# A two-layer convolution kernel: expert products placed ahead in the first image, Newton square roots, a second chunk buffer, and small moves in four queues

## The chip, the cores and the metric

One Trainium2 chip, one of its cores. The number that counts is the device time of one execution in microseconds, the median of several runs of the same program. A profile is one further execution, recorded instruction by instruction; its own time is given beside its span.

## The reference, cut to what matters

The input `x` has the shape (4, 64, 256, 256): four images of 64 channels. Everything is float32.

```python
# layer 0, on the group norm of x (32 groups, per image)
h = gelu(conv3x3(x)); xa, k = split(conv1x1(h))
xs = gelu(conv3x1(conv1x3(xa)))                    # one filter for each channel
mask = top2(softmax(mean(xs) @ gate_w.T))          # per image, three experts
out = xs + sum_i mask[i] * c1x1(c1x1(k) * c1x1(xs)) # inner widths 2, 4, 8
x = x + conv1x1(out)
# layer 1, on the group norm of the new x (per image)
h = relu(batchnorm(conv3x3(x, quantized w1)))      # statistics over all four images
h = batchnorm(conv3x3(h, quantized w2))
x = x + relu(h + identity)
```

The quantized weights are scaled by the largest absolute weight over 127, rounded, clipped and scaled back. A group norm divides by the square root of a variance; there are eight of these in all (four images in each layer), and two batch norms.

## The kernel before, in words

**Stages.** The program runs through them once: statistics of image 0 (to about 52 us of the span); the *front* of layer 0 for 64 units of 16 rows, 16 units for each image (57 to about 1310 us, the last units overlapping the next stage); the first convolution of layer 1, in 64 chunks of 8 row pairs, called conv1 (1271 to 1960 us); batch norm; the second convolution (1970 to 2520 us); and an end stage that only streams (to 2958 us). PE is the matrix engine, DVE the vector engine, ACT the scalar engine, POOL the fourth compute engine. DMA transfers are issued by SP and, for a few stores, by ACT.

**An order written by hand.** `at(step, order, call)` puts a call into a table, and the table is executed sorted by `(step, order)`; every engine, SP's queue among them, keeps that order. `at_slot(u, pos, call)` is the same in slots: slot `u` is two steps, and `pos` runs from 0 to 12 within it. So a position in the table fixes where an instruction stands among the others of its own engine; when it runs is decided by the waits. A chain such as `stats_end` is a generator: each `next` in the table runs it to its next `yield`.

**One slot of the front.** PE does, in this order: products (1, 2) and (3, 4) of the transformed convolution (pos 1 and 1.3, `front_conv`, 24 + 24 matmuls, tile `ps_c`, two buffers); the first rounds of the taps of unit u-2 (pos 2, `front_taps_a`, tile `ps_a`, one buffer); their last rounds (pos 4, `front_taps_b`); products (0, 5) into the bank of (3, 4) (pos 5); the first rounds of unit u-1 (pos 7); in even slots `front_k` and in odd slots `front_q` (pos 8, tiles `ps_k` and `ps_q`, in the one buffer of tag "p"); the last rounds of unit u-1 (pos 9). Each `front_taps_b` waits for a memset, called the tick (`divide`, L506), which waits for the last matmul of the `front_taps_a` before it. The tick is on DVE in image 0 and on POOL afterwards.

The other engines' part of a slot: DVE combines the products (`butterfly_a` to `_d`, L631 to L650; `butterfly_c`, pos 4.05, has to be done before products (0, 5) are added to its bank), finishes the taps (`front_taps_h`, L706, L714, L717; the last of them frees `ps_a`), and takes half of the next image's statistics in image 0 (`stats_group`, `bn_stats`, L415). ACT copies and scales (L547, L570, L572, L626), starts the taps (L699), applies gelu (L658, L730), and takes the rest of the statistics (`stats_piece`, L448). POOL makes the input transform (L553 to L596).

From slot 20 on (`u >= NCH + 4`) the output of the image before runs in the same slots: tiles `y` (two buffers) are loaded from `in_xp`, added to, and stored to `y_d`. There `ps_o` also needs tag "p".

**Layer 1's weights** are quantized on DVE in `weights1`, a chain of three parts, for `w1` in slots 7 to 9 and for `w2` in slots 10 to 12, at pos 7.3. The middle part holds three operations on 128x768 (L253, L254, L255).

**Square roots.** `combine` averages over a group by two small matmuls and ends with Sqrt on ACT (L282) and a reciprocal on DVE (L284). It is called by `stats_end` (layer 0's norm), `group_norm` in `out_end` (layer 1's norm) and `bn_affine`.

**conv1.** For each chunk: `conv1_load` (tile `yn`, by SP), differences on POOL (L343), upper and lower halves on ACT and DVE (L930, L359, L346; L362, L353), 36 matmuls (`ps_hm`, `ps_h`, L296), the result on DVE (`leave`, L318), squares on ACT (L382) and a store of the result to `h1_d` by ACT's queue (L998). The result tile is `h1` of `conv1_pool`, one buffer, or, for odd chunks from the fourth on, the place of `chunk_x`. The output of image 2's last third and of image 3 runs beside conv1 (`plan_out_late`): `out_slot` about every fourth step, and `out_store` (L893) by SP one step after each second `out_slot`. The last slots of the front (`TAIL`) run beside the first chunks.

## Time and profile before

| | us |
|---|---|
| median of 3 runs | 2964.82 |
| lowest, highest | 2963.71, 2973.92 |
| the profiled execution | 2959.65 |
| its span, first to last instruction | 2957.8 |
| PE, DVE, ACT, POOL busy | 2345.4, 2448.4, 2007.1, 1676.8 |

The profiled execution lies 5.2 us below the median of the runs. A busy share is an average over stages with different limits; what a change in one stage is worth is read in that stage. In the timeline rows a line gives start, duration, engine, line of the source and the tiles written and read; brackets give the idle time of the engine before it and what ended that. In the table by stretch each engine's busy time stands beside the length of the stretch.

### The profile page before, as it was taken

To read this page: it belongs to the slowest core of one execution; us is meant where nothing else is said; L and a number is where in the kernel's file an instruction comes from. 1 tells how busy PE (TensorE), PEld (TensorE's weight loads), DVE (VectorE), ACT (ScalarE), POOL (GpSimd) and SP (SyncE) were. 2 spreads that over 40 slices of the span, in tenths; PEclk is the share of its full clock that TensorE was granted. 3 is DMA by queue.
4 is the path that set the end of the run, shared out by engine and by line. 5 is a ranking of instruction groups with operands and counts; after the bars stand their busy time and mean duration, and the time that the engine had idled before them with its cause. 6 is when DMAs were issued, how large, how long until landed. Compare 5 with 4: busy or idle time off the path is not lost.

```text
span 2957.8 us, 52737 instructions
## 1 busy us (share of the span) xinstructions
PE 2345.4 (79%) x21576; PEld 1502.1 (51%) x21576; DVE 2448.4 (83%) x2811; ACT 2007.1 (68%) x2183; POOL 1676.8 (57%) x1252
## 2 busy tenths in 40 slices
PE   2888899999999999979999999989999999000000
PEld 1444445444445555546666667867788888000000
DVE  6688678888888988869999999979999898976664
ACT  4777888787776665567676667978888887432221
POOL 6988888787778888733545546735555555000000
PEclk9999999999999999999999999999999999555555
DMA  8665579999999999859999997747777764999999
GB/s 352 233 239 209 199 269 369 354 351 350 355 349 320 320 319 327 290 203 320 343 367 361 332 360 272 270 176 274 258 267 264 270 219 156 375 412 423 420 424 409
DMA packets 135715, 915.35 MB, mean 309 GB/s; under 512 B 14960, under 2 KB 15728, under 8 KB 40880
## 3 DMA queue, kind: packets, MB, share of 16 engines
q1 hardware_dynamic: 107824, 777.74, 71.1%
q10 hardware_dynamic: 27648, 134.23, 11.3%
q8 instruction: 170, 2.79, 0.4%
q14 instruction: 73, 0.60, 0.1%
HBM read 573.74 MB, written 338.17 MB: 308 GB/s over the span
## 4 chain that ended last, share of the span: by engine, by line
PE 50%; DMA 29%; DVE 13%; ACT 3%; POOL 2%; issue 2%; SPq 0%; ACTq 0%; DVEq 0%; POOLq 0%
PE ps_h L296 18%; PE ps_c L513 9%; DMA y<-in_xp 7%; PE ps_a L513 7%; PE ps_h2m L296 6%; DMA y_end<-y_d 5%; DMA y_d<-y 4%; DMA out<-h 4%; DMA h<-h_d 4%; PE ps_o L513 4%; DMA yn<-y_d 3%; PE ps_hm L296 3%; DVE t L714 2%; DVE t L717 2%; PE ps_k L744 1%
## 5 line engine op out<-in xcount | busy, mean ns | idle before, releaser
L296 PE MATMUL ps_h<-diff,w_q 128*128 128x512 f32 x3072 | 755.2, 400 | 12.4 <-DVE h L318 11.9
L296 PEld LDWEIGHTS ps_h<-diff,w_q 128*128 128x128 f32 x3072 | 577.0, 189 | 190.6 <-issue 20.4
L513 PE MATMUL ps_c<-v,us 64*64 64x256 f32 x9216 | 534.0, 380 | 28.6 <-DVE ps_c L644 25.4
L343 POOL TENSOR_TENSOR d<-yn 128x1024 f32<-128x1024 f32 x128 | 348.9, 2745 | 299.3 <-DMA yn<-y_d 164.8
L513 PEld LDWEIGHTS ps_c<-v,us 64*64 64x64 f32 x9216 | 360.7, 134 | 174.4 <-issue 17.6
L343 POOL TENSOR_TENSOR d<-h 128x1024 f32<-128x1024 f32 x126 | 307.1, 2459 | 206.4 <-DVE diff L351 143.6
L513 PE MATMUL ps_a<-h,av 64*64 64x512 f32 x4080 | 386.5, 492 | 47.3 <-DVE t L717 40.1
L318 DVE SCALAR_TENSOR_TENSOR h<-ps_h,scale_w,m 128x1024 f32<-128x1024 f32 x256 | 323.1, 1279 | 78.7 <-PE ps_h L296 56.3
L561 POOL TENSOR_TENSOR x<-x 128x512 f32<-128x512 f32 x256 | 328.8, 1284 | 12.7
L1497 ACT ACTIVATE h<-h,shift,gn 128x2048 f32<-128x2048 f32 (+1 forms) x65 | 134.3, 2067 | 276.0 <-DVE h L1496 273.8
L513 PEld LDWEIGHTS ps_a<-h,av 64*64 64x64 f32 x4080 | 153.7, 133 | 322.2 <-issue 212.8
L382 ACT ACTIVATE junk<-h,less_h 128x2048 bf16<-128x2048 f32 (+3 forms) x134 | 256.2, 1912 | 13.6 <-DVE h L318 13.5
L1496 DVE SCALAR_TENSOR_TENSOR h<-h,inverse,y_end 128x2048 f32<-128x2048 f32 (+1 forms) x65 | 150.5, 2317 | 122.0 <-DMA y_end<-y_d 122.0
L699 ACT ACTIVATE t<-ps_a,tap_bias,m 128x1016 f32<-128x1016 f32 x128 | 153.3, 1197 | 117.0 <-PE ps_a L513 91.4
L880 DVE SCALAR_TENSOR_TENSOR y<-ps_o,ob,y 128x1024 f32<-128x1024 f32 x128 | 164.0, 1281 | 50.9 <-PE ps_o L513 26.6
L730 ACT ACTIVATE xs<-t 128x1024 f32<-128x1024 f32 x128 | 134.8, 1053 | 103.8 <-DVE t L717 90.2
L353 DVE SCALAR_TENSOR_TENSOR diff<-d,gn,diff 128x1024 fp32r<-128x1024 f32 x128 | 202.0, 1608 | 0.9 <-ACT diff L346 0.5
L296 PE MATMUL ps_h2m<-odd,w_q 128*128 128x512 f32 x768 | 193.5, 401 | 5.9 <-ACT odd L359 3.8
L296 PE MATMUL ps_hm<-odd,w_q 128*128 128x512 f32 x768 | 194.0, 402 | 2.8 <-DVE t L717 1.3
L346 ACT ACTIVATE diff<-d 128x1024 fp32r<-128x1024 f32 x128 | 135.3, 1057 | 81.1 <-POOL d L343 79.5
L553 POOL TENSOR_TENSOR x<-x,x 128x512 f32<-128x512 f32 x128 | 160.5, 1275 | 34.2 <-ACT x L547 34.2
L717 DVE SCALAR_TENSOR_TENSOR t<-ps_a,m,t 128x1020 f32<-128x1020 f32 x128 | 163.9, 1280 | 4.6
(256 smaller groups left out, 4235.2 us busy)
## 6 DMA issues: line engine op xcount, KB each, us to landing
x<-in_xc SPq DMA_DIRECT2D x64, 1280.0 KB
h<-h_d SPq DMA_DIRECT2D x64, 1152.0 KB
yn<-y_d SPq DMA_DIRECT2D x60, 1152.0 KB
xs_in<-in_xp SPq DMA_DIRECT2D x64, 1024.0 KB
xs_d<-xs ACTq DMA_DIRECT2D x128, 512.0 KB
xs_in<-xs_d SPq DMA_DIRECT2D x64, 1024.0 KB
y<-in_xp SPq DMA_DIRECT2D x64, 1024.0 KB
y_d<-y SPq DMA_DIRECT2D x64, 1024.0 KB
```

The lines of the kernel that those rows point to most:

```text
L296: nc.tensor.matmul(ps, wq[w][:, kind, kx, :], t[:, rows, kx : kx + W], start=(j == 0), stop=(j == len(terms) - 1))
L318: nc.vector.scalar_tensor_tensor(h.rearrange("p (e k) w -> p e (k w)", e=2), ps.rearrange("p e k w -> p e (k w)"), w_scale[w], m.unsqueeze ...
L343: engine.tensor_tensor(raw.rearrange("p (g r) w -> p g r w", g=2), *pair, ALU.subtract)
L353: nc.vector.scalar_tensor_tensor(lower, raw, scale, upper.bitcast(F32), ALU.mult, ALU.subtract)
L382: nc.scalar.activation(junk[rows, 0:n], flat(h), AF.Square, bias=less[name][rows], accum_out=total)
L513: last[:] = [nc.tensor.matmul(ps[o, at_out[0] : at_out[1], :], w[i], rhs[i], **flags)]
L553: nc.gpsimd.tensor_tensor(x4[:, j - 1], x_rows(u, j + 2), x4[:, j - 1], ALU.subtract)
L561: nc.gpsimd.tensor_tensor(x[:, r : r + 2], x[:, r + 2 : r + 4], x[:, r : r + 2], ALU.subtract)
L699: nc.scalar.activation(t[:, :, inside], ps[:, :, inside], AF.Identity, bias=tap_bias, scale=sh[:, 1:2])
L717: nc.vector.scalar_tensor_tensor(t[:, :, 0 : W - 1], ps[:, :, 1:W], sh[:, 2:3], t[:, :, 0 : W - 1], ALU.mult, ALU.add)
L880: nc.vector.scalar_tensor_tensor(y, ps.rearrange("p x s w -> p x (s w)"), out_bias[b], y, ALU.add, ALU.add)
L1496: nc.vector.scalar_tensor_tensor(at_h, at_h, inverse[:, b : b + 1], y[:, a:e, :], ALU.mult, ALU.add)
```

## The change

It has seven parts.

1. In slots below 20, `front_k` stands at 4.5, between `front_taps_b` and products (0, 5), instead of 8; three quarters of `front_q` (units 0 to 2) stand at 4.5 too, and the last quarter stays at 8.
2. In image 0 the first `bn_stats` pair of a slot stands at 6.125 (behind `butterfly_d`) instead of 4.1.
3. `weights1` yields after each of its three large operations; it runs in slots 5 to 8 (`w1`) and 9, 10, 11, 14 (`w2`).
4. For images 1 to 3 of layer 0's norm and all four of layer 1's, the square root and reciprocal become a first guess on DVE (two operations, one of them on the bits as an integer) and three Newton steps of three operations each on POOL. Image 0's norm and the batch norms keep Sqrt. The chains get one more place each, and some places move.
5. Chunk 1 of image 0 in conv1 writes its result to the place of `chunk_x` too.
6. For that chunk, `conv1_upper` and the first `conv1_lower` stand behind the front's taps of the same step.
7. `out_store` of the late output stands two steps after its `out_slot`, not one.

```diff
@@ weights1
         nc.vector.reciprocal(inv, scale)
-        yield
         nc.vector.tensor_scalar(w, w, inv, ROUND, ALU.mult, ALU.add)
+        yield
         nc.vector.tensor_scalar(w, w, ROUND, None, ALU.subtract)
+        yield
         nc.vector.tensor_scalar(w, w, QMAX, -QMAX, ALU.min, ALU.max)
         yield
@@ new, and its call in combine
+    HALF = 0.5
+    MAGIC = 1597463007.0
+    def root(var, n, y, name):
+        nc.vector.tensor_scalar(var, var, 1.0 / n, eps, ALU.mult, ALU.add)
+        nc.vector.tensor_scalar(y.bitcast(I32), var.bitcast(I32), -HALF, MAGIC, ALU.mult, ALU.add)
+        t = stat.tile([P, 1], F32, tag="ct", name=f"root_{name}")
+        for _ in range(3):
+            yield
+            nc.gpsimd.tensor_scalar(t, var, y, y, ALU.mult, ALU.mult)
+            nc.gpsimd.tensor_scalar(t, t, -HALF, 1.0 + HALF, ALU.mult, ALU.add)
+            nc.gpsimd.tensor_tensor(y, y, t, ALU.mult)
...
+        if step:
+            yield from root(var, n, out[:, 1:2], name)
+            return
         yield
         nc.scalar.activation(var, var, AF.Sqrt, bias=eps_t, scale=1.0 / n)
@@ front_q
-    def front_q(b, j):
+    def front_q(b, j, units=range(4)):
...
-            for i in range(4):
+            for i in units:
@@ conv1_out
-            if k % 2 and (b > 0 or k > 2):
+            if k % 2:
@@ plan_front
+            alone = u < NCH + 4
-                at_slot(u, 8, front_k, *divmod(j, NOCT // 4))
+                at_slot(u, 4.5 if alone else 8, front_k, *divmod(j, NOCT // 4))
...
-                at_slot(u, 8, front_q, *divmod(j, NOCT // 4))
+                if alone:
+                    at_slot(u, 4.5, front_q, *divmod(j, NOCT // 4), range(3))
+                at_slot(u, 8, front_q, *divmod(j, NOCT // 4), range(3 if alone else 0, 4))
...
-            for n in range(3):
-                at_slot(7 + 3 * i + n, 7.3, next, chain, None)
+            for u in ((5, 6, 7, 8), (9, 10, 11, 14))[i]:
+                at_slot(u, 7.3, next, chain, None)
@@ plan_stats
-                at_slot(int(s), 4.1 if s - int(s) < 0.5 else 7.25, stats_group, b, *group)
+                early = 6.125 if int(s) < NCH else 4.1
+                at_slot(int(s), early if s - int(s) < 0.5 else 7.25, stats_group, b, *group)
...
-        places = (e, 8.3), (e + 1, 1.25), (e + 1, 1.36), (e + 2, 1.25), (e + 2, 1.36), (e + 2, 4.45), (e + 2, 8.3), (e + 3, 1.25), (e + 3, 1.36)
+            (e, 6.126 if b == 1 else 8.3), (e + 1, 1.25), (e + 1, 1.36), (e + 2, 1.25), (e + 2, 1.36),
+            (e + 2, 5.6), (e + 2, 7.4), (e + 3, 2.45), (e + 4, 1.25), (e + 4, 1.36),
@@ plan_out_late
-                at(step + 1, 13.3, out_store, b, n // 2)
+                at(step + 2, 13.3, out_store, b, n // 2)
@@ plan_conv1
+            behind = b == 0 and k == 1
-            at(*late(up0, 13.12), conv1_upper, b, k, 0)
-            at(*late(up1, 13.14), conv1_upper, b, k, 1)
+            at(*late(up0, 13.36 if behind else 13.12), conv1_upper, b, k, 0)
+            at(*late(up1, 13.37 if behind else 13.14), conv1_upper, b, k, 1)
...
-            at(*((t, 1.3) if first else late(low0, 13.22)), conv1_lower, b, k, 0)
+            at(*((t, 1.3) if first else late(low0, 13.45 if behind else 13.22)), conv1_lower, b, k, 0)
```

More of the change, by code (lines that the diff above doesn't have):

```diff
@@ L12 @@
 BF16 = mybir.dt.bfloat16
+I32 = mybir.dt.int32
 AF = mybir.ActivationFunctionType
@@ L251, in weights1 @@
         nc.vector.reciprocal(inv, scale)
+        nc.vector.tensor_scalar(w, w, inv, ROUND, ALU.mult, ALU.add)
         yield
-        nc.vector.tensor_scalar(w, w, inv, ROUND, ALU.mult, ALU.add)
         nc.vector.tensor_scalar(w, w, ROUND, None, ALU.subtract)
+        yield
         nc.vector.tensor_scalar(w, w, QMAX, -QMAX, ALU.min, ALU.max)
@@ L261, in weights1, with combine @@
         nc.vector.tensor_scalar(wq[name][:, 2], second, -1.0, None, ALU.mult)
-    def combine(mv, n, avg, eps_t, out, name, engine=nc.vector):
+    HALF = 0.5
[9 more added lines that the diff above has]
+            nc.gpsimd.tensor_tensor(y, y, t, ALU.mult)
+    def combine(mv, n, avg, eps_t, out, name, engine=nc.vector, step=False):
         mean = out[:, 0:1]
@@ L289, in group_norm @@
         yield
-        yield from combine(mv, 1, avg, eps, out, name, engine)
+        yield from combine(mv, 1, avg, eps, out, name, engine, True)
     def convolve(ps, w, kind, tiles, rows):
@@ L484, in stats_end @@
         yield
-        yield from combine(mv, n, c128("avg4"), eps, own, f"x{b}", nc.vector if b == 0 else nc.gpsimd)
+        yield from combine(mv, n, c128("avg4"), eps, own, f"x{b}", nc.vector if b == 0 else nc.gpsimd, b > 0)
         if b == 0:
@@ L758, in front_k_out @@
         nc.scalar.activation(flat(k_sb[b, j]), ps.rearrange("p s f -> p (s f)"), AF.Identity, bias=k_bias)
-    def front_q(b, j):
-        ps = ps_q[b, j] = bank("p", f"ps_q_{b}_{j}").rearrange("p s a b -> p s (a b)")
+    def front_q(b, j, units=range(4)):
+        if 0 in units:
+            ps_q[b, j] = bank("p", f"ps_q_{b}_{j}").rearrange("p s a b -> p s (a b)")
+        ps = ps_q[b, j]
         for s in range(2):
-            for i in range(4):
+            for i in units:
                 x = xss[b, 4 * j + i][:, s]
@@ L1175, in plan_stats @@
                 s = slots[k] + group[2] // 2 * per / 2
-                at_slot(int(s), 4.1 if s - int(s) < 0.5 else 7.25, stats_group, b, *group)
+                early = 6.125 if int(s) < NCH else 4.1
+                at_slot(int(s), early if s - int(s) < 0.5 else 7.25, stats_group, b, *group)
         e = NCH * b - 4
-        places = (e, 8.3), (e + 1, 1.25), (e + 1, 1.36), (e + 2, 1.25), (e + 2, 1.36), (e + 2, 4.45), (e + 2, 8.3), (e + 3, 1.25), (e + 3, 1.36)
+        places = (
+            (e, 6.126 if b == 1 else 8.3), (e + 1, 1.25), (e + 1, 1.36), (e + 2, 1.25), (e + 2, 1.36),
+            (e + 2, 5.6), (e + 2, 7.4), (e + 3, 2.45), (e + 4, 1.25), (e + 4, 1.36),
+        )
         chain = stats_end(b)
@@ L1202, in plan_out @@
             chain = out_end(b)
-            for place in ((e + 1, 8.35), (e + 2, 1.25), (e + 2, 1.36), (e + 3, 1.25), (e + 3, 1.36), (e + 3, 4.45), (e + 3, 8.3)):
+            for place in ((e + 1, 8.35), (e + 2, 1.25), (e + 2, 1.36), (e + 3, 1.25), (e + 3, 1.36), (e + 3, 5.6), (e + 3, 7.4), (e + 4, 2.45)):
                 at_slot(*place, next, chain, None)
@@ L1276, in conv_preact_kernel @@
             if b == B - 2:
-                plan_out_late(b, range(22, NOCT), [CONV1 + 16 + 4 * n for n in range(10)], 13.6, [(CONV1 + n, 12.6) for n in (56, 58, 58, 60, 60, 60, 62)])
+                plan_out_late(b, range(22, NOCT), [CONV1 + 16 + 4 * n for n in range(10)], 13.6, [(CONV1 + n, 12.6) for n in (56, 58, 58, 60, 60, 60, 61, 62)])
         else:
@@ L1280, in conv_preact_kernel @@
             steps = [t + (e - 6 - t) * n // (NOCT - 1) for n in range(NOCT)]
-            plan_out_late(b, range(NOCT), steps, 13.6, [(e - i, 15) for i in (5, 3, 3, 1, 1, 1, -1)])
+            plan_out_late(b, range(NOCT), steps, 13.6, [(e - i, 15) for i in (5, 3, 3, 1, 1, 1, 0, -1)])
         plan_conv1(b)
```

## The prediction, made before the changed kernel was run

> **What bounds the kernel now.** I read the busy shares first, then the table by stretch for image 0's slots, then timelines of single slots and of the places that the diff touches.
>
> ```profile
> span 2957.8 us, 52737 instructions
> PE 2345.4 (79%) x21576; PEld 1502.1 (51%) x21576; DVE 2448.4 (83%) x2811; ACT 2007.1 (68%) x2183; POOL 1676.8 (57%) x1252
> ```
>
> No engine is full over the whole. Parts 1 to 3 act on image 0's slots only (57 to about 410 us):
>
> ```profile
> core 0: us, PE busy (x) PEld busy (x) DVE busy (x) ACT busy (x) POOL busy (x), PEclk, DMA share, GB/s
> 120.08:282.34 162.26, 141.33 (x2081) 76.66 (x2081) 133.00 (x197) 123.16 (x170) 139.35 (x110) 1.00 0.63 222
> 282.34:338.81 56.47, 48.70 (x711) 25.92 (x711) 37.26 (x58) 48.59 (x69) 48.50 (x48) 1.00 0.56 206
> 338.81:410.45 71.64, 63.64 (x926) 33.88 (x926) 50.02 (x69) 64.56 (x91) 62.63 (x66) 1.00 0.61 211
> ```
>
> The first row holds nine slots of 18.03: per slot PE 15.70, POOL 15.48, DVE 14.78, ACT 13.68. PE is granted its full clock and DMA has room, so PE's gaps count; but POOL would be full at nearly the same length. The gaps, in one slot:
>
> ```profile
> 118.66 0.66 PE L513 MATMUL ps_a<-h,av 64*64 64x256 f32 x8 [0.23 <-DVE tick_v L506]
> 119.24 0.69 DVE L644 SCALAR_TENSOR_TENSOR ps_c<-d,ps_c 128x512 f32<-128x512 f32 x1
> 119.85 1.28 DVE L415 BATCH_NORM_STATS2 st_x<-xs_in 128x6 f32<-128x512 f32 x2
> 120.08 2.82 PE L513 MATMUL ps_c<-v,us 64*64 64x256 f32 x48 [0.77 <-DVE ps_c L644]
> 122.61 1.28 DVE L717 SCALAR_TENSOR_TENSOR t<-ps_a,m,t 128x1020 f32<-128x1020 f32 x1
> 124.04 2.38 PE L513 MATMUL ps_a<-h,av 64*64 64x512 f32 x24 [1.13 <-DVE t L717]
> 126.35 1.92 PE L766 MATMUL ps_q<-xs,m 128*32 128x512 f32 x16
> ```
>
> PE stops for 0.77 us ahead of (0, 5), until DVE's L644 is done, and for 1.13 us ahead of the next taps, until L717 frees `ps_a`; L717 is late because the `bn_stats` pair (1.28) stands ahead of it. With the tick, 15.6 + 0.23 + 0.77 + 1.13 is about the slot's 17.75.
>
> **Part by part.**
>
> *Products ahead, and `bn_stats` behind (parts 1, 2).* I count from the end of the earlier last rounds of the taps (119.32). Before, (0, 5) starts at +0.77. After, k (1.88) or three quarters of q (1.92 x 3/4 = 1.44) runs there first, inside the wait, and (0, 5), 2.82 long, ends at +4.7 or +4.3. DVE: L706 follows ACT's L699 (+0.07 to +1.27) at once; 0.22 + 1.28 + 1.28 and small gaps make L717 end at +4.15, `ps_a` free at about +4.3. The taps then start at +4.7 or +4.3, not +4.72 with k still to come: both gaps go. Later, the last rounds start at +7.15 instead of +8.9, so at most 1.75 per slot is gained. Against it: without k there, the tick waits in even slots for the moved `bn_stats` pair (DVE until about +6.9), estimated 0.25. PE alone would give 16.0 to 16.3. The covers are thin: POOL has 15.48 of work, its `v` sums wait for (0, 5), now 0.7 to 1.1 later, and ACT holds about 16.1 in odd slots (the rows of a slot added up, k's copy of 1.1 being in even ones). I take 16.8, between PE's 16.1 and a slot that keeps most of the waits, 17.3. Nine slots: 162.26 - 9 x 16.8 = 11.1 gained; the slot before them, 1.
>
> *The weights (part 3)* and *image 0's root.*
>
> ```profile
> 271.01 1.51 DVE L254 TENSOR_SCALAR mset<-mset 128x768 f32<-128x768 f32 x1
> 272.56 0.56 DVE L255 TENSOR_SCALAR mset<-mset 128x768 f32<-128x768 f32 x1
> 321.59 1.28 ACT L282 ACT_TABLE_LOAD   x1
> 322.88 0.29 ACT L282 ACTIVATE var_x<-var_x,eps 128x1 f32<-128x1 f32 x1
> 323.20 1.28 ACT L730 ACT_TABLE_LOAD   x1
> ```
>
> The three operations of 128x768 (0.97 + 1.51 + 0.56 = 3.04) stood together in one slot for each weight; the slot with w2's is 19.93 long, 1.9 above its fellows. Spread, the sum is the same, but no slot takes more than about 1.5: included in the 16.8. L254 and L255 are the same kind and size: 1.51 while POOL works, 0.56 while it idles. The Trainium skill, "SBUF — State Buffer", section "SBUF: two separate sides", says why this can speak against the change: VectorE and GpSimd share a port pair that is an exclusive lock. By the row, each spread operation costs at most 1.5 on DVE; by the rule, each of the six may also wait for a whole POOL operation (1.28) and hold one back, in slots where POOL no longer has slack. By the row the sum stays; by the rule it loses 2 to 3 us. I take the row, and keep 3 in the range.
>
> The root in slot 318.76 to 338.81 (20.05 long): 1.28 + 0.29 + 1.28 = 2.9 on ACT, gone. The Trainium skill, "ScalarE: Activation LUTs", section "What ACT_TABLE_LOAD costs", adds a drain of about 1.38 us to each load of 1.28, 5.3 for a pair; here the operations follow the loads within 0.04 us, so 2.9 is used (the rule would add 2.4). In exchange come two tiny DVE operations and nine tiny ones on POOL (0.2 to 0.3 each by nearby rows of 128x1), some 2.4 on POOL in three pieces, spread over two slots. The three slots of the second row: 56.47 to 3 x 17.1, 5.2 gained. The four of the third row have no `bn_stats` or weights, but part 1: 71.64 to 4 x 17.3, 2.4 gained.
>
> Front sum: 1 + 11.1 + 5.2 + 2.4 = 19.7, between 10 (17.3 everywhere and no better) and 26 (PE's floor).
>
> *The other seven roots.* Five lie in slots of images 1 to 3 of about 20 us, with DMA the bound (its share is .96 to 1.00 there), two beside conv1 where ACT is not last. Their loads were hidden. -1, bounded by +2 (63 tiny POOL operations by 0.25 are 16 us over long stretches in which POOL idles) and -4. The first batch norm's Sqrt now has to load its table again, 1.28; ACT is idle 2.9 us ahead of that place: nothing, 1.28 if it isn't.
>
> *The start of conv1 (parts 5, 6).*
>
> ```profile
> 1278.82 2.82 DVE L353 SCALAR_TENSOR_TENSOR diff<-d,gn,diff 128x1024 fp32r<-128x1024 f32 x1 [0.54 <-ACT diff L346]
> 1284.55 0.98 PE L513 MATMUL ps_a<-h,av 64*64 64x512 f32 x4 [3.35 <-DVE t L717]
> 1318.60 1.21 ACT L312 ACTIVATE m<-ps_hm,m,scale_w 128x1024 f32<-128x1024 f32 x1 [5.86 <-DMA low_d<-k]
> 1318.68 0.33 ACTq L998 DMA_DIRECT2D h_d<-h  x1
> 1330.17 1.28 DVE L318 SCALAR_TENSOR_TENSOR h<-ps_h,scale_w,m 128x1024 f32<-128x1024 f32 x1 [12.49 <-DMA h_d<-h]
> 1331.52 0.79 PE L296 MATMUL ps_h<-diff,w_q 128*128 128x512 f32 x1 [8.57 <-DVE h L318]
> ```
>
> The first two lines: PE waits 3.35 for L717, which stands behind the first L353 (2.82) of chunk 1. Behind the taps, that goes in part: -2.3. The others: chunk 2's result shares the one buffer of chunk 1's, whose store was issued at 1318.68 and landed at 1330. DVE waits 12.49, and PE, with nowhere to put products, 8.57. With a place of its own for chunk 1, chunk 2's L318 waits only for L312, done at 1319.8. The next things late are the loads issued at 1316 to 1319 (`yn` and `ranks`), which land at some 1329 to 1333 by their issue-to-landing times, and chunk 3's result, waiting for the same store at 1330. After this, PE has work in hand again, so I count -8 of PE's 8.57 to 10 of DVE: -10 for both parts, between -13 and -4.
>
> *Stores a step later (part 7).* No compute moves. In SP's queue, the next `yn` load goes ahead of the store in image 3's late output (from about 1600 us):
>
> ```profile
> 1603.93 0.33 SPq L835 DMA_DIRECT2D y<-in_xp  x1
> 1614.01 0.32 SPq L893 DMA_DIRECT2D y_d<-y  x1
> 1614.49 0.32 SPq L912 DMA_DIRECT2D yn<-y_d  x1
> 1619.95 5.73 POOL L343 TENSOR_TENSOR d<-yn 128x1024 f32<-128x1024 f32 x2 [11.45 <-DMA yn<-y_d]
> ```
>
> SP stands at the store until DVE has finished the last add, with the `yn` load behind it; POOL then starves 11.45. Five such chunks are 12 to 16 us long where 10.5 is usual, some 14 us together. A load that goes ahead removes a part where it was not late for want of bandwidth. -4, between -9 and +4.
>
> **Sum.** -19.7 - 1 - 10 - 4 = -34.7: 2959.65 - 34.7 = 2925 for the profiled execution. The median of the runs lay 5.2 above it: 2930.
>
> **The rivals.**
>
> 1. *Slower: the output ring.* `y` has two buffers. A load takes 14 to 21 us, the two adds about 12, the store 9 to 17, of a period of some 42. If, ahead of the store, SP now stands in the `yn` load's own wait for a free `yn` buffer, and that ends later than the add does, each store, and the next `y` load behind it, slips. From 2.6 us of slip on, the next add is late, and DVE with it; 12 chunks by 5 us are +60 against -30 elsewhere: 2990. For it: waits of SP at `yn` loads of 5 to 9 us occur. Against: the buffer it asks for was released about 18 us before.
> 2. *POOL, ACT and DVE close up.* If image 0's slots go only to 17.3 (POOL's chain after (0, 5) as long as before), the front gives 8 instead of 19.7: 2942. For it: 15.48 of POOL in 16.8. Against: it is idle 2.5 per slot, and reaches ahead through its buffers.
> 3. *conv1's wait only moves.* Chunk 2 waits for `ranks` or `yn` until 1331 whatever buffer it has, and the place of `chunk_x` is itself late. Then parts 5 and 6 bring 2, not 10: 2938. For it: issue times 1316 to 1319 and landings near 1330. Part 5 then doesn't do what it says.
>
> **How the numbers follow.** My sum has a chance of 0.57, with its own range 2914 to 2946; the second rival 0.16; the third 0.12; the first 0.09; the rest (0.06) lies on both sides of no change. The bounds of the terms (-10 to -26, -4 to +2, -4 to -13, +4 to -9, the lock's 3) do not all fall one way; root of squares is about 13 each way, to which the second rival adds above. The range is 2907 to 2960. 0.5%, about what a measurement of this kernel can tell from no change, is 14.8 us: below 2950 is faster (nearly all of 0.57, three quarters of the second and third rival: 0.76), above 2980 slower (0.10), between 0.14.
>
> **What would show it.** In image 0, (0, 5) without the 0.77 for L644 and the taps without the 1.13 for L717; (0, 5) to (0, 5) about 16.8 instead of 18.03; no table load between 60 and 1310 us; the slot at 319 like its fellows. In conv1, L318 of chunk 2 without its 12.49, and no PE gap of 8 us there; `yn` loads ahead of L893 after 1600, with POOL's waits for `yn` shorter. Wrong would be: waits for POOL's `v` on PE in image 0, slots of 17.3 or more; a new wait of DVE at 1320 to 1331 for `ranks`; SP standing at L912 with the store behind it.

## The result, and the profile after

| | before | after |
|---|---|---|
| median of 6 runs of each | 2973.6 us | 2945.38 us |
| lowest, highest | 2963.71, 2975.74 | 2935.38, 2952.13 |
| span of the profiled execution | 2957.8 | 2933.5 |

The ratio is 0.9909 (95% interval 0.9882 to 0.9936): 0.9% faster, about 27 us. On another chip the same two kernels gave 2973.67 and 2939.73, ratio 0.9892 (0.9874 to 0.9910). The forecast of 2930 had the direction and the order of size; the measured gain is some 8 us smaller than the 34.7 of its sum, and in the two profiled executions, which are compared from here on, 24.3.

In the changed kernel a line of the source stands some 20 lower than before: L644 is now L663, L717 is L736, L318 is L337, L343 is L362, L893 is L914, L912 is L933.

First the busy times of the page:

```profile
PE 2353.0 (80%) x21576; PEld 1500.6 (51%) x21576; DVE 2435.1 (83%) x2818; ACT 1992.5 (68%) x2166; POOL 1693.0 (58%) x1315
```

Then the table by stretch for the same slots of image 0 as before (nine, three, and the four split into the first and the other three):

```profile
core 0: us, PE busy (x) PEld busy (x) DVE busy (x) ACT busy (x) POOL busy (x), PEclk, DMA share, GB/s
117.80:270.26 152.46, 148.30 (x2104) 77.27 (x2101) 131.28 (x198) 122.56 (x170) 138.05 (x109) 1.00 0.66 240
270.26:322.30 52.04, 49.40 (x697) 26.04 (x689) 36.70 (x57) 44.07 (x65) 46.99 (x51) 1.00 0.54 207
322.30:342.42 20.12, 17.97 (x249) 8.73 (x246) 12.82 (x19) 17.37 (x25) 18.64 (x21) 1.00 0.57 217
342.42:396.35 53.93, 48.79 (x691) 25.17 (x683) 37.85 (x54) 48.34 (x69) 47.92 (x53) 1.00 0.61 207
```

The nine slots went from 162.26 to 152.46, that is 16.94 a slot. PE is busy for 148.30 of it: it is the bound there now. But its busy time *rose*, by 7 us, though the change adds no arithmetic; that is taken up below. The first of the last four slots takes 20.12.

The slot that the prediction shows at 120.08, after the change, from the timeline: three quarters of q stand ahead of (0, 5), and neither (0, 5) nor the next taps carries a bracket, so PE waits for neither; L736 ends at 120.2, before the taps begin at 120.45. The even slots look the same, with k in the place of q.

```profile
115.95 1.92 PE L787 MATMUL ps_q<-xs,m 128*32 128x512 f32 x12
117.80 2.82 PE L532 MATMUL ps_c<-v,us 64*64 64x256 f32 x48
118.91 1.28 DVE L736 SCALAR_TENSOR_TENSOR t<-ps_a,m,t 128x1020 f32<-128x1020 f32 x1
120.45 2.32 PE L532 MATMUL ps_a<-h,av 64*64 64x512 f32 x24
122.70 1.90 PE L787 MATMUL ps_q<-xs,m 128*32 128x512 f32 x4
```

At conv1's start, chunk 2's result waits 2.15 for L331 (L312 before) instead of 12.49 for the store, and PE goes on to the next products without a gap:

```profile
1301.32 1.28 DVE L337 SCALAR_TENSOR_TENSOR h<-ps_h,scale_w,m 128x1024 f32<-128x1024 f32 x1 [2.15 <-ACT m L331]
1304.25 5.82 PE L315 MATMUL ps_h<-diff,w_q 128*128 128x512 f32 x24
```

Before, PE not only waited 8.57 there. The products behind the wait ran slowly, 7.94 us for the same 24 matmuls, at a mean granted clock of 0.72 (a row of the timeline before, and one of the table by stretch):

```profile
1331.52 7.94 PE L296 MATMUL ps_h<-diff,w_q 128*128 128x512 f32 x24 [8.57 <-DVE h L318]
1331.52:1339.46 7.94, 7.94 (x27) 6.29 (x27) 7.90 (x8) 6.65 (x7) 3.02 (x2) 0.72 1.02 196
```

Wait and clock together are 10.7 us; chunk 3, from one `ps_hm` to the next, went from 19.57 to 8.71.

In the late output, SP issues the next `yn` load ahead of the store:

```profile
1582.64 0.44 SPq L933 DMA_DIRECT2D yn<-y_d  x1
1592.61 0.32 SPq L914 DMA_DIRECT2D y_d<-y  x1
```

**Where the time went.** I compare the start of the same matmuls in both traces: products (0, 5) of a slot in the front, `ps_hm` of a chunk in conv1. The lead of the changed kernel grows or shrinks by these amounts in each stretch:

| stretch | forecast | profile |
|---|---|---|
| to the slot at 97.8 (no part acts yet, but for half of one slot) | 0 | 1.6 |
| image 0's slots, 97.8 to 410 | 19.7 | 12.6 |
| images 1 to 3, to 1243 | 1 | 1.9 |
| to chunk 4 of conv1 | 10 | 13.4 |
| chunks 4 to 16 | 0 | -7.4 |
| chunks 16 to 46 | 4 | 6.3 |
| chunks 46 to 50 | 0 | -3.7 |
| from there to the end | 0 | -0.4 |
| sum | 34.7 | 24.3 |

The first row differs between kernels that are the same up to that point (-1.1 to +1.6), so it is the scatter of a start. The chunks' lengths below are from one `ps_hm` to the next.

### The profile page after: what moved, and what is told of

It reads as the page before. It is cut to its first block, busy times and chain, and to the rows that moved or that the text cites. A ratio compares the mean times of both kernels' runs of the same rounds, so it can differ in the third digit from the quotient of the medians.

```text
span 2933.5 us, 52776 instructions
## 1 busy us (share of the span) xinstructions
PE 2353.0 (80%) x21576; PEld 1500.6 (51%) x21576; DVE 2435.1 (83%) x2818; ACT 1992.5 (68%) x2166; POOL 1693.0 (58%) x1315
## 4 chain that ended last, share of the span: by engine, by line
PE 48%; DMA 31%; DVE 11%; POOL 4%; ACT 3%; issue 2%; SPq 0%; ACTq 0%; DVEq 0%; POOLq 0%
PE ps_h L315 18%; PE ps_c L532 9%; DMA y<-in_xp 7%; DMA y_d<-y 6%; PE ps_h2m L315 6%; PE ps_a L532 6%; DMA y_end<-y_d 5%; DMA h<-h_d 4%; DMA out<-h 4%; PE ps_o L532 4%; PE ps_hm L315 3%; DMA yn<-y_d 3%; PE ps_q L787 1%; POOL x L580 1%; DVE y L901 1%
## 5 line engine op out<-in xcount | busy, mean ns | idle before, releaser
L532 PE MATMUL ps_c<-v,us 64*64 64x256 f32 x9216 | 535.0, 380 | 13.8 <-DVE ps_c L663 11.3
L362 POOL TENSOR_TENSOR d<-yn 128x1024 f32<-128x1024 f32 x128 | 347.4, 2735 | 277.2 <-DMA yn<-y_d 181.1
L532 PEld LDWEIGHTS ps_c<-v,us 64*64 64x64 f32 x9216 | 358.7, 134 | 170.3 <-issue 15.8
L362 POOL TENSOR_TENSOR d<-h 128x1024 f32<-128x1024 f32 x126 | 307.7, 2464 | 206.5 <-DVE diff L370 136.9
L337 DVE SCALAR_TENSOR_TENSOR h<-ps_h,scale_w,m 128x1024 f32<-128x1024 f32 x256 | 323.2, 1280 | 73.6 <-PE ps_h L315 59.3
L749 ACT ACTIVATE xs<-t 128x1024 f32<-128x1024 f32 x128 | 134.8, 1053 | 104.0 <-DVE t L736 93.9
L372 DVE SCALAR_TENSOR_TENSOR diff<-d,gn,diff 128x1024 fp32r<-128x1024 f32 x128 | 192.7, 1536 | 0.0
L315 PEld LDWEIGHTS ps_h2m<-odd,w_q 128*128 128x128 f32 x768 | 146.4, 191 | 42.6 <-ACT odd L378 3.9
```

What stands on the lines that cost most here:

```text
L315: nc.tensor.matmul(ps, wq[w][:, kind, kx, :], t[:, rows, kx : kx + W], start=(j == 0), stop=(j == len(terms) - 1))
L337: nc.vector.scalar_tensor_tensor(h.rearrange("p (e k) w -> p e (k w)", e=2), ps.rearrange("p e k w -> p e (k w)"), w_scale[w], m.unsqueeze ...
L362: engine.tensor_tensor(raw.rearrange("p (g r) w -> p g r w", g=2), *pair, ALU.subtract)
L372: nc.vector.scalar_tensor_tensor(lower, raw, scale, upper.bitcast(F32), ALU.mult, ALU.subtract)
L532: last[:] = [nc.tensor.matmul(ps[o, at_out[0] : at_out[1], :], w[i], rhs[i], **flags)]
```

## The experiments

Twelve runs. Each was timed beside the kernel before on the same chip; "lead" is against the profiled execution before, as in the table. The changed kernel itself was timed again on the chip of e9_both, e10_half_store and e12_bn_early alone (e11_after); the other comparisons with it go from chip to chip, and so both by the medians and by the ratios to before.

### Parts 1 and 2 alone (e1_image0)

```diff
-                at_slot(u, 8, front_k, *divmod(j, NOCT // 4))
+                at_slot(u, 4.5 if alone else 8, front_k, *divmod(j, NOCT // 4))
...
+                    at_slot(u, 4.5, front_q, *divmod(j, NOCT // 4), range(3))
...
+                early = 6.125 if int(s) < NCH else 4.1
```

> The kernel before with parts 1 and 2 alone (k and three quarters of q ahead of products (0, 5); the first statistics pair behind butterfly_d). Theory: in image 0, PE is the bound once its two waits are gone, so these two parts make the slots: 16.9 us a slot from (0, 5) to (0, 5), as in the changed kernel, some 9 us gained over the nine slots to 282 us without any of the other parts, and about 10 faster than before at the end of the front. At the end of the program 6 to 10 faster, since the stretches that DMA fills give some of it back. Rival (POOL, ACT and DVE close up; the weights and the square root are what makes the slots long): slots of 17.4 or more, 5 or less gained. In both, q's last quarter shows a row as long as that of its first three (1.9 us each).

2969.16 against 2968.56 before, ratio 0.9997 (0.9983 to 1.0011): no gain. The reason is in the slots: seven of the nine are as in the changed kernel (17.4 and 15.8 to 16.7 by turns), but the two that hold a weight's operations are not. The slot at 256 takes 22.0 us, and the nine take 158.92, 3.3 less than before. The theory was right for the slots without weights and wrong in that part 1 would carry the gain without part 3: the sum is the rival's (17.66 a slot on average). In the profile, the lead of 3.3 at 410 us was then lost in slots 28 to 43, where an output runs beside the front and DMA is full.

### Weights in one slot again (e6_weights)

```diff
-            for u in ((5, 6, 7, 8), (9, 10, 11, 14))[i]:
-                at_slot(u, 7.3, next, chain, None)
+            for n in range(3):
+                at_slot(7 + 3 * i + n, 7.3, next, chain, None)
```
(and the yields of `weights1` as before)

> The changed kernel with layer 1's weights as before: each weight's three operations of 128x768 in one slot (part 3 undone). Theory: without slack in image 0's slots, three operations in a row on DVE (about 4 us) hold back the end of the taps and PE's next ones; the slot with w2's becomes about 22 us instead of 17.4, that with w1's about 18.3 instead of 16.4: 6 to 7 us lost by 290 us, and 4 to 7 us at the end. Rival (the sum of DVE's work is the same, so it costs what it cost before, 1.9 in one slot): 2 us lost.

2950.91 against 2966.38, ratio 0.9939 (0.9912 to 0.9966). The slot with w2's takes 23.16 us instead of 17.43, that with w1's 18.26 instead of 16.40, and the nine slots 160.03 instead of 152.46: 7.6 us, which are not made up (at the last chunk the lead is 14.4 instead of 24.7; at the end 17.4, the end stage being 3 us shorter in this profile). The timeline shows the mechanism: three operations of 0.96 to 1.52 stand ahead of the end of the taps in DVE's queue, and PE's next taps wait. They are also slow: the granted clock over them is 0.50 (the last row, of the table by stretch).

```profile
261.95 0.96 DVE L254 TENSOR_SCALAR mset<-mset,inv_w 128x768 f32<-128x768 f32 x1
262.95 1.52 DVE L255 TENSOR_SCALAR mset<-mset 128x768 f32<-128x768 f32 x1
264.50 1.51 DVE L256 TENSOR_SCALAR mset<-mset 128x768 f32<-128x768 f32 x1
...
271.12 4.55 PE L531 MATMUL ps_a<-h,av 64*64 64x512 f32 x24 [2.84 <-DVE t L735]
271.12:275.67 4.55, 4.55 (x24) 1.40 (x24) 2.43 (x4) 1.99 (x3) 2.48 (x2) 0.50 0.99 345
```

Before the change the three of w2 cost their slot 1.9; with PE's own waits gone they cost 5.7. Of these, 2.84 are the wait and 2.2 the slow taps behind it. Before, the wait at this place was 1.86, and the taps kept their 2.38:

```profile
278.24 2.38 PE L513 MATMUL ps_a<-h,av 64*64 64x512 f32 x24 [1.86 <-DVE t L717]
```

Nor is DVE's sum the same. All six operations of 128x768 took 7.5 us before, 8.0 in this run and 5.1 in the changed kernel, where each stands alone in its slot and takes 0.62 to 0.98. POOL works beside them in all three.

### q whole at its old place (e7_q_whole)

```diff
-                if alone:
-                    at_slot(u, 4.5, front_q, *divmod(j, NOCT // 4), range(3))
-                at_slot(u, 8, front_q, *divmod(j, NOCT // 4), range(3 if alone else 0, 4))
+                at_slot(u, 8, front_q, *divmod(j, NOCT // 4))
```

> The changed kernel with q whole at its old place (behind the later first rounds of the taps), k still ahead of products (0, 5). Theory: q's four units run side by side, one to each 32 columns of PE, so three of them take as long as four (1.92 us) and the last one alone 1.90 more; the split fills two waits of 0.77 and about 0.7 in an odd slot and costs 1.90, so it brings nothing: two slots together take 33.8 us with it and 33.5 to 34.0 without, and the time stays within 2 us of the changed kernel. Rival (three quarters cost three quarters, the sum of the prediction): without the split two slots take 0.8 to 1.5 us more, and the time is 7 to 13 us above the changed kernel.

2943.03 against 2966.38, ratio 0.9922 (0.9895 to 0.9950), which is where the changed kernel stands. The first eight of the nine slots take 134.96, against 135.03: splitting q brings nothing, as the theory had it. (All nine take 153.69, against 152.46; but this stretch ends with an odd slot, which here holds all of q.) The rows say why. The changed kernel's two parts of q, then the whole one here, in its slot with the two waits that the split had filled (timelines of PE):

```profile
217.16 1.92 PE L787 MATMUL ps_q<-xs,m 128*32 128x512 f32 x12
...
223.91 1.90 PE L787 MATMUL ps_q<-xs,m 128*32 128x512 f32 x4
```

```profile
218.98 2.82 PE L532 MATMUL ps_c<-v,us 64*64 64x256 f32 x48 [0.86 <-DVE ps_c L663]
222.43 2.38 PE L532 MATMUL ps_a<-h,av 64*64 64x512 f32 x24 [0.62 <-DVE t L736]
224.74 1.92 PE L787 MATMUL ps_q<-xs,m 128*32 128x512 f32 x16
```

Sixteen matmuls of 32 columns take 1.92 us, twelve take 1.92, and four take 1.90. The four units are written to four different groups of 32 output rows. The Trainium skill, "TensorEngine Tiling (Array Packing)", sections "Available Configurations" and "Key Properties", has the rule: in the 128 by 32 form the array is four independent tiles that work side by side. Three of four cost as much as four, so the split costs 1.9 of PE's time in each odd slot, and the waits that it fills are worth 0.86 + 0.62 and the offsets of pipelining around them. In the stretch of nine slots, nine pieces of q stand where five whole ones stood before: four more, 7.6 us, which is about the 7 us by which PE's busy time rose. Over the whole program PE is busy for 2340.9 us here and for 2353.0 in the changed kernel.

### Both products ahead, both whole (e8_kq_shift)

```diff
 for j = 1 to 7:
+                    at_slot(2 * j + 3, 4.5, front_k, ...)     # k one slot later
+                    at_slot(2 * j + 4, 4.5, front_q, ...)     # q whole, one slot later
+        tag, bufs = ("ranks", 2) if b == 0 and n % 4 == 0 else ("xs", 4)
```

> The changed kernel with another placing of k and q in image 0: k of units 2j, 2j+1 ahead of products (0, 5) of the odd slot 2j+3, and q whole ahead of products (0, 5) of the next even slot, for j from 1 to 7 (one tile in four of xs gets another place, since they live a slot longer). Theory: PE is the bound of these slots, and each wait is filled by work that is there anyway, so a slot takes its 15.7 us of matmuls and two ticks of 0.23: 16.2 instead of 16.9, some 7 to 10 us less than the changed kernel by slot 17 and 5 to 9 at the end. Rival (POOL at 15.4 us of work and ACT are as near their limit): 16.7 or more a slot, and no more than 3 us gained.

2940.41 against 2966.38, ratio 0.9915 (0.9881 to 0.9949). In the slots the theory held: 16.35 and 16.13 by turns where this placing is in force, and PE has no wait but the ticks (here q, whole, in place of the wait).

```profile
167.13 0.66 PE L532 MATMUL ps_a<-h,av 64*64 64x256 f32 x8 [0.53 <-DVE tick_v L525]
167.72 1.93 PE L788 MATMUL ps_q<-xs,m 128*32 128x512 f32 x16
169.57 2.82 PE L532 MATMUL ps_c<-v,us 64*64 64x256 f32 x48
```

So POOL, ACT and DVE would allow 16.2 a slot. The nine slots gain another 3.5 us (148.98), and the last four lose 2.7 (76.75 instead of 74.05); but in runs with the same front as the changed kernel these four take 74.1 to 77.5, so the loss need not be the placing's. In the time it can't be told from the changed kernel.

### The first statistics pair at its old place (e12_bn_early)

```diff
-                early = 6.125 if int(s) < NCH else 4.1
+                early = 4.1
```

> The changed kernel with the first statistics pair of a slot at its old place, ahead of the end of the taps (part 2 undone). Theory: the work placed ahead of products (0, 5) takes 1.9 us in every slot, in odd ones too, so PE comes to the next taps only 4.7 us after the end of the earlier ones, and L736 is done by then even behind the pair (4.57): a slot stays 16.9 on average, and the front within 1.5 us of the changed kernel; part 2 brings nothing once part 1 is there. Rival (the prediction: L736 0.4 earlier counts in each slot): 0.3 to 0.5 a slot more, 3 to 5 us by 282 us.

2953.31 against 2967.77, ratio 0.9939 (0.9916 to 0.9961). In image 0, nine slots take 154.79, 2.3 more than in the changed kernel, all but 0.3 of it in the five odd ones (17.8 to 17.9 instead of 17.42). That lies between the two expectations: in odd slots PE waits 0.21 for L736 after all. Most of the rest of the loss in the profile arose where part 2 does nothing: 10.0 in slots 28 to 43 (569 to 869 us in the changed kernel) and 8.1 in the end stage; see the end.

### Sqrt everywhere again (e5_all_sqrt)

```diff
-        if step:
-            yield from root(var, n, out[:, 1:2], name)
-            return
```
(in effect; and the places of the chains as before)

> The changed kernel with Sqrt on ACT for all of the norms (part 4 undone). Theory: the square root of image 0's slots costs ACT 2.9 us and returns to the slot in which it stood: one of the slots between 306 and 345 us is 2 to 3 longer; the roots of images 1 to 3 make no difference in the front, and those beside conv1 cost nothing on ACT but hold POOL when they are Newton steps, so chunks 47 and 48 go back to about 17.7 us together. Net: within 3 us of the changed kernel. Rival (the roots carry the gain, as the prediction had it): 5 us or more above the changed kernel.

2944.61 against 2966.38, ratio 0.9932 (0.9914 to 0.9951). The slot at 309 takes 20.17 instead of 16.34, but the one after it 17.79 instead of 20.12; image 0's slots together are 2.1 longer, not 5. Beside conv1 the loss that the Newton steps cause (next run) is not there either, so that, from the slot at 117.8 to the last chunk, the lead grows by 22.5 here and by 22.4 in the changed kernel: part 4 as a whole brings nothing that shows. In the time this run is 1 us below the changed kernel by the medians and 7 above it by the ratios; in its profile the end stage alone is 5.4 longer. The loads and the root between them are the same rows as before, with gaps of 0.04 at most:

```profile
310.71 1.28 ACT L301 ACT_TABLE_LOAD   x1
312.00 0.29 ACT L301 ACTIVATE var_x<-var_x,eps 128x1 f32<-128x1 f32 x1
312.32 1.28 ACT L749 ACT_TABLE_LOAD   x1
```

In the changed kernel the late place of the end of the Newton chain moves the work that hangs on it into the next slot. Its timeline there:

```profile
326.43 2.38 PE L532 MATMUL ps_a<-h,av 64*64 64x512 f32 x24 [1.31 <-DVE t L736]
327.06 1.25 ACT L487 ACTIVATE us<-u_raw,gn 128x1152 f32<-128x1152 f32 x1 [1.36 <-POOL gn L277]
329.41 1.90 PE L787 MATMUL ps_q<-xs,m 128*32 128x512 f32 x4 [0.59 <-ACT xs L749]
```

ACT waits for POOL's last step, scales image 1's weights (1.25), is late with xs, and q's last quarter waits 0.59 for it.

### Sqrt again beside conv1 only (e2_late_sqrt)

```diff
-        yield from combine(mv, 1, avg, eps, out, name, engine, True)
+        yield from combine(mv, 1, avg, eps, out, name, engine, step)   # step: b < B - 2
```

> The changed kernel with Sqrt on ACT again for the two norms whose end lies beside conv1 (layer 1's norm of images 2 and 3); the other five chains keep the Newton steps. Theory: there the nine small operations on POOL hold back the differences of the next chunks in POOL's queue (POOL waited 7.2 us for DVE's first guess, with two chunks' differences queued behind, and chunks 47 and 48 took 11.7 and 10.0 us where they took 9.2 and 8.5 before). So chunks 47 and 48 go back to about 17.7 together, chunk 15 to 12.8 from 14.2, and the time is 4 to 6 us under that of the changed kernel, about 32 under before. Rival: these chunks wait for their yn loads, whatever POOL does: no difference beyond 1 us to the changed kernel (about 27 under before).

2938.33 against 2968.56, ratio 0.9895 (0.9879 to 0.9911). Chunks 47 and 48 take 9.17 and 8.49: the 3.7 us that the changed kernel loses between chunks 46 and 50 are not lost here. POOL's timeline, first in the changed kernel, then here:

```profile
1778.67 0.34 POOL L275 TENSOR_SCALAR root_y<-var_y,gn 128x1 f32<-128x1 f32 x1 [7.17 <-DVE gn L271]
...
1781.53 2.24 POOL L939 TENSOR_SCALAR yn<-zeros,gn 128x256 f32<-128x256 f32 x1
1783.85 10.89 POOL L362 TENSOR_TENSOR d<-yn 128x1024 f32<-128x1024 f32 x4
```

```profile
1779.97 0.93 POOL L939 TENSOR_SCALAR yn<-zeros,gn 128x256 f32<-128x256 f32 x1 [4.81 <-DVE gn L286]
1780.98 5.54 POOL L362 TENSOR_TENSOR d<-yn 128x1024 f32<-128x1024 f32 x2
```

With Newton steps, POOL waits for DVE's first guess, does nine small operations, and only then the differences of two chunks that stood behind. With Sqrt it waits for a mean that comes earlier, and does the first two differences meanwhile. In all of the runs, the four kernels with Sqrt at this place lose nothing between chunks 46 and 50, and the nine with Newton steps lose 3.1 to 3.7. Chunk 15, where image 2's norm ends, shows the same: it takes 14.1 to 14.8 in the nine with Newton steps, and 11.3 to 13.3 in the four with Sqrt and in the kernel before. In the changed kernel the last of the three steps stands on POOL behind differences of 4.75 us, DVE waits for it, and PE waits for DVE:

```profile
1450.97 0.22 DVE L924 TENSOR_SCALAR gn<-gn 128x1 f32<-128x1 f32 x1 [5.67 <-POOL gn L277]
1452.44 0.99 PE L315 MATMUL ps_h_end<-diff,w_q 128*128 128x256 f32 x6 [1.26 <-DVE h L337]
```

This wait of PE's, 1.26 to 2.77 us, stands in seven of the nine, and in none with Sqrt. For the whole time, the gain over the changed kernel (7 by the medians, 4 by the ratios) is within what the runs can tell.

### Parts 5 and 6 undone (e3_no_place)

```diff
-            if k % 2:
+            if k % 2 and (b > 0 or k > 2):
-            behind = b == 0 and k == 1
+            behind = False
```

> The changed kernel without parts 5 and 6: chunk 1's result in the one buffer again, and its upper and lower halves ahead of the front's taps. Theory: the parts gain 13 us at chunk 4 (DVE's wait of 12.5 us for the store comes back), but chunks 4 to 16, where DMA is at 0.91 to 0.98 of its time, give half of that back; so without them the lead over before at chunk 4 is some 13 us smaller than in the changed kernel, at chunk 16 only some 5 to 7 smaller, and the time at the end is 5 to 7 us above the changed kernel. Rival: the lead that the changed kernel loses between chunks 4 and 16 is lost to the stores or the Newton steps there and not to DMA: then this kernel loses as much there too, and ends 12 to 13 us above the changed kernel.

2952.65 against 2968.56, ratio 0.9947 (0.9931 to 0.9963), 7 us above the changed kernel by the medians, 11 by the ratios. The wait of DVE is back (12.57 for the store of `h_d`), and between chunks 0 and 4 nothing is gained, where the changed kernel gains 14.8: 3.9 in chunk 0 (part 6) and 10.9 in chunk 3 (part 5). But this kernel also loses nothing between chunks 4 and 16, where the changed one loses 7.4. At chunk 16 the two leads are 15.7 and 22.0, as the theory had it; the time at the end lies between the two expectations.

### Fewer bytes beside chunks 2 to 13 (e10_half_store)

```diff
+        if b == 0 and 2 <= k <= 13:
+            nc.scalar.dma_start(h1_d[b][:, first half of the chunk], h[:, : CPAIR // 2, :])
+            return
+        if b == 3 and 2 <= k <= 13:
+            nc.scalar.dma_start(h1_d[0][:, second half of the chunk], h[:, CPAIR // 2 :, :])
```

> The changed kernel, with half of each result store taken out of chunks 2 to 13 of conv1 (0.5 of 1 MB each) and as many bytes stored beside chunks 50 to 61 instead, where DMA has room; what conv2 then reads for those rows is not the convolution's result. Theory: the lead that the changed kernel loses between chunks 4 and 14 (4.6 us of 29.4, chunks 9 to 13 taking 10.6 to 13.3 where 10.5 is usual) is lost to DMA, full at 0.91 to 0.98; with 6 MB less there, some 17 us of its time, chunks 5 to 13 all take 10.5 to 10.6 and the lead at chunk 14 is 28 or more. Rival (SP's order or the chain of the norm's end makes those waits): the chunks are as long as in the changed kernel, and the lead at chunk 14 is 23 to 25 again.

2930.04 against 2973.67, ratio 0.9856 (0.9834 to 0.9879), from two executions, and of a kernel that leaves half of those results out of their place, so not a version to use. Chunks 5 to 13 take 10.52 to 10.54, all of them, and the lead at chunk 14 is 28.8, as at chunk 4. Chunks 4 to 13 of the changed kernel, then of this one, in the table by stretch:

```profile
1310.04:1352.53 42.49, 42.29 (x211) 28.98 (x210) 40.22 (x55) 32.70 (x33) 19.96 (x8) 1.00 0.98 348
1352.53:1419.99 67.46, 63.83 (x313) 43.33 (x312) 61.08 (x64) 45.46 (x44) 32.60 (x13) 1.00 0.94 335
```

```profile
1310.65:1352.86 42.21, 42.21 (x211) 28.96 (x210) 40.17 (x56) 32.46 (x33) 21.24 (x9) 1.00 0.85 294
1352.86:1416.04 63.18, 63.18 (x313) 43.31 (x312) 60.72 (x63) 46.35 (x44) 31.73 (x13) 1.00 0.94 322
```

PE is then busy from end to end (63.18 of 63.18). So the time between chunks 4 and 14 is lost to DMA: it was at 0.98 in the first of these stretches, a `yn` load landed late, and POOL waited 15.96 for it, to 1385.46, where in this run it waits 12.54, to 1380.78. That an earlier start of conv1 asks for its bytes while those of the front are still under way is the likely reason; no run shows which transfers were in the way.

### The store one step later, undone (e4_store)

```diff
-                at(step + 2, 13.3, out_store, b, n // 2)
+                at(step + 1, 13.3, out_store, b, n // 2)
```

> The changed kernel with the late output's store one step after its out_slot again (part 7 undone). Theory: a store that stands in SP's queue ahead of the next yn load holds that load back, and chunks of 11 to 14 us where 10.5 is usual come back at chunks 41, 44 and 45; the time is 3 to 6 us above the changed kernel, all of it between chunks 16 and 46. Rival: the long chunks wait for bandwidth, DMA being at 0.9 to 0.97 there, and only move to other chunks: no difference beyond 2 us.

2949.25 against 2968.56, ratio 0.9944 (0.9923 to 0.9966), 4 above the changed kernel by the medians, 10 by the ratios. Between chunks 16 and 46 the lead falls by 3.8, where it grows by 6.3 in the changed kernel. Chunk 41 takes 17.61 (chunks 44 and 45, also expected to be long, take 10.52 and 9.97); the `yn` load stands behind the store in SP's queue, and POOL waits (SP and POOL, timeline):

```profile
1735.49 0.32 SPq L914 DMA_DIRECT2D y_d<-y  x1
1735.91 0.37 SPq L933 DMA_DIRECT2D yn<-y_d  x1
...
1743.78 4.71 POOL L362 TENSOR_TENSOR d<-yn 128x1024 f32<-128x1024 f32 x2 [11.80 <-DMA yn<-y_d]
```

In all, the two kernels without part 7 beside the one before change their lead there by -5.6 (e1_image0) and -3.8 (this one), and the eleven with it by -0.1 to +6.3, ten of them by +2.4 or more: the mean is 4.2. So part 7 is worth some 4 us against the profile before, and up to 10 against the other two. But the kernel before and e1_image0, with the same instructions there, lie 5.6 apart, so the size stays uncertain.

### Both repairs, and the changed kernel again (e9_both, e11_after)

```diff
 e9_both: the edits of e8_kq_shift and e2_late_sqrt together; e11_after: none
```

> The changed kernel with the two improvements together: k and q of image 0 shifted by a slot, both ahead of products (0, 5), and Sqrt again for layer 1's norms of images 2 and 3. Theory: the two lie in different stages, so the gains add up as far as DMA lets them: some 3 to 5 in image 0 and 4 at chunks 47 and 48, 5 to 9 us under the changed kernel on the same chip, about 32 to 36 under before. Rival (the stretches that DMA fills take all of it back): within 3 us of the changed kernel.

> The changed kernel again, as it is, for a comparison with the others on one chip: 24 to 30 us under before; both theories say the same.

2943.54 and 2939.73, before 2973.67 on the same chip; ratios 0.9891 (0.9869 to 0.9912) and 0.9892 (0.9874 to 0.9910). The two repairs do in their stages what they did alone: nine slots take 149.02, and nothing is lost between chunks 46 and 50. Yet the time is not better. In the profile of e9_both, slots 28 to 43, with an output beside the front, take 12 us more (the changed kernel, then e9_both, in the table by stretch):

```profile
569.07:868.63 299.56, 283.33 (x3981) 145.48 (x3976) 250.93 (x329) 232.68 (x327) 240.76 (x258) 1.00 0.97 355
```

```profile
569.42:881.17 311.75, 288.61 (x3980) 146.72 (x3976) 250.11 (x329) 232.90 (x327) 241.23 (x258) 0.98 0.95 341
```

The bytes are the same (355 x 299.56 = 341 x 311.75 = 106.3 thousand KB each), moved more slowly. PE is also busy for 5.3 us more, at a mean granted clock of 0.98; which of the two led to the other was not separated. One of its six runs came to 2927.42, the others to 2940 to 2946. No version that computes the same beats the changed kernel by more than the scatter.

## Why the forecast was right, and where its sum was off

- *PE's waits in image 0 go.* Right: 16.94 a slot against 16.8, nine slots 9.8 us instead of 11.1. But the working behind it was partly wrong: "three quarters of q (1.92 x 3/4 = 1.44)". A part of q costs all of q, and the split brings nothing (e7_q_whole). The 16.8 came out about right because the other three engines, which the sum had put close to their limit, allow 16.2 (e8_kq_shift): two errors offset, which is luck.
- *"POOL, ACT and DVE close up" (second rival).* Not so in the end, but DVE's queue does close up if the weights stay together. "Included in the 16.8" under-priced part 3: it is worth 7.6 us once part 1 is there, and without it parts 1 and 2 are worth nothing that the runs can tell. Two terms were missing: the clock behind a longer wait of PE, and DVE's sum, which does not stay the same but falls from 7.5 to 5.1. The reading that was to settle it was wrong: POOL did not idle beside the 0.56 of L255 before; its L587 ran from 272.61, 0.05 us after L255 began, to 274.26. The exclusive lock that spoke against the spreading did not show as a loss: beside the spread operations POOL's take 1.47 to 1.49 us, against 1.26 to 1.28 for the ones just ahead.
- *Image 0's root: 5.2 in three slots, 2.4 in the last four.* Three slots gave 4.4, the last four lost 2.4. Newton steps instead of Sqrt, with the places that go with them, are worth 2.1. The failed step is that the 2.9 us of table loads were taken off one slot without asking where the chain's end goes: its last POOL operations, and ACT's scaling behind them, fall into the next slot. The duration itself was right; the drain that the Trainium skill, "ScalarE: Activation LUTs", section "What ACT_TABLE_LOAD costs", adds to a load was not seen in e5_all_sqrt either. The sign "no table load between 60 and 1310 us" could not come: the loads for Sqrt are gone, but the pairs of L822 and L749, near 380, 693 and 1004, stay (L801 and L730 before).
- *The other seven roots.* They are six, for seven roots change in all (63 / 9), one of them in image 0's slots: four in images 1 to 3 and two beside conv1. The stretch of the four gained 1.9, but 4.2 with Sqrt (e5_all_sqrt), so no gain of theirs shows; two of them lie where DMA's share was 0.91, and PE, not DMA, was full.
- *"63 tiny POOL operations ... over long stretches in which POOL idles".* Their sum was right (POOL is busy for 16.2 us more), and still this step failed: beside conv1 POOL idles because it waits, with chunks behind it in its queue, and others wait for the steps in turn. 3.7 us at chunks 46 to 50, and some 1.4 at chunk 15.
- *conv1's start: -10.* It gave 13.4, a little above its range's end of 13: part 6 3.9 instead of 2.3, and part 5 10.9 instead of 8, because the wait of 8.57 had a slow clock behind it, 2.1 more, which the sum did not hold (1.4 were lost ahead of chunk 0, as in most of the runs, also in e1_image0, which has neither part); `ranks` and `yn`, which the third rival expected late at 1331, were not. What failed is the next clause, "after this, PE has work in hand again": half of it, 7.4, is given back by chunk 16, mostly because DMA is full there. e10_half_store shows the cause of the part up to chunk 14 (4.6); the rest (2.8) is half chunk 14, 19.05 us instead of 17.64, which is back at 17.13 in e10_half_store, and half chunk 15, which goes with the Newton steps of image 2's norm.
- *The store a step later: -4.* 6.3 in the profile, 4.2 on the mean of the runs. The output ring of the first rival never became late.
- *The median.* The profiled execution before lay 5.2 below the first three runs' median and 14.0 below that of six; the changed kernel's 10.0 below its own. The offset of 5.2 was too small a sample.

## What to carry to other kernels

Before a wait is filled with work from elsewhere, look at what a part of that work costs: matmuls on four column groups are cheap only when all four run together. When an engine's own waits go, everything else in the slot loses its cover, so a term that cost 1.9 before (three weight operations in a row) can cost 5.7 after, the slower clock behind the longer wait included. And a lead gained ahead of a stretch with DMA at 0.95 or more is only partly kept; price that stretch too, and a small operation by what stands behind it in its queue, not by its own length.

## What the runs showed of the hardware beyond the question

Behind two of its longer waits PE ran at a lower granted clock: 0.50 over the 24 matmuls behind a wait of 2.84 in e6_weights, which took 4.55 us instead of 2.38, and 0.72 over those behind 8.57 in the kernel before. Behind a wait of 1.86 the same taps kept their 2.38. No run varied the length of the wait, so where the line lies is open; but these two waits cost three quarters and a quarter more than their brackets say.

With DMA at 0.95 to 0.97 of its time, the same 106 MB of slots 28 to 43 took 298 to 312 us, 341 to 356 GB/s, from one kernel to another, with the same transfers in the same order there. The changed kernel's two profiles gave 299.6 and 301.2, before 301.4, e1_image0 306.8, e12_bn_early 309.5, e9_both 311.8. The end stage, with DMA full (a share of 0.99 to 1.00) and the same instructions, took 436.3 to 447.4 us in the fourteen profiles, at 416 to 406 GB/s. Each of the two is as much as several parts of the change together, and both would explain runs of one kernel that lie up to 23 us apart; a single profile's span or final lead says little for the same reason. Whether a kernel's timing provokes it or each execution draws it was not settled, with one profile of each.

A small operation on POOL can take four times its length: between 1441.67 and 1443.04, L275 on 128x1 took 1.37 us, beside a DVE addition of two tensors from 1441.68 to 1442.91, and 0.34 a microsecond earlier. The Trainium skill, "SBUF — State Buffer", section "SBUF: two separate sides", names an exclusive lock between the two engines, held also by a DVE operation with two inputs in SBUF, and taken by whichever of the two starts first. These rows agree in that POOL's operation ends only after DVE's, though by its row it began 0.01 us earlier; no run varied it.

```profile
1440.67 0.34 POOL L275 TENSOR_SCALAR root_y<-var_y,gn 128x1 f32<-128x1 f32 x1 [4.55 <-DVE gn L271]
1441.67 1.37 POOL L275 TENSOR_SCALAR root_y<-var_y,gn 128x1 f32<-128x1 f32 x1
1441.68 1.23 DVE L381 TENSOR_TENSOR odd<-yn,odd 128x1024 fp32r<-128x1024 f32 x1
```
